# Cross-attention of a perceiver block: row maxima through DRAM, combines of four units, no fills, and masks divided anew among the engines

## The chip, the cores and the metric

The kernel runs on one core of one Trainium2 chip. The metric is device time in microseconds (us). Four runs of the kernel before gave 1000.0, 1001.75, 1003.12 and 1005.47 us; their median is 1002.43. One more execution was profiled.

The engines go by the profile's names: PE is TensorE's matrix multiplication and PEld its loads of the stationary operand, DVE is VectorE, ACT is ScalarE, POOL is GpSimd, SP is SyncE, which here only issues DMAs. "SPq" and "POOLq" are DMA issues of SP and POOL. L916 is line 916 of the kernel before.

## The reference

The program runs a perceiver's two layers in float32: in the first layer a cross-MLP, an attention and a mixture of experts, in the second a cross-attention, an attention by Fourier transforms and a layer of expert heads. The change is in the second layer's cross-attention and at its edges:

```python
# x (2, 256, 256), ctx (2, 4096, 256), mask (1, 1, 256, 4096)
def _L1_xattn_ref(values, keys, queries, mask, w_out, b_out):
    EMBED, HEADS, HEAD_DIM = 256, 16, 16
    v = values.reshape(N, -1, HEADS, HEAD_DIM)      # values = keys = ctx
    k = keys.reshape(N, -1, HEADS, HEAD_DIM)
    q = queries.reshape(N, -1, HEADS, HEAD_DIM)     # queries = layernorm(x)
    energy = jnp.einsum('nqhd,nkhd->nhqk', q, k)
    energy = jnp.where(mask == 0, jnp.float32(-1e+20), energy)
    attn = jax.nn.softmax(energy / math.sqrt(EMBED), axis=3)
    out = jnp.einsum('nhql,nlhd->nqhd', attn, v).reshape(N, q_len, HEADS * HEAD_DIM)
    return out @ w_out.T + b_out
```

So there are 2 x 16 independent softmaxes of 256 queries over 4096 keys, with a head dimension of only 16.

## The kernel before

**Units and steps.** One batch and one head make a unit (`UNITS`, 32 of them). A unit has 4096 keys, held transposed in a tile `keys` of 128 rows: four groups of 32 rows, each with 1024 keys; the group's rows 0 to 15 hold the 16 dimensions of the head and its rows 16 to 31 hold ones. There are five such tiles, filled with ones by POOL at L849, and `load_keys` writes the 16 rows of each group by four DMAs of SP (L857). The queries of a unit lie in a slot of `q0` in the same way, four copies in rows 0 to 15 of the four groups and zeros below (the fill is L869, the DMAs are L884); there are four slots, used in turn. Both loads are made two units ahead, at step 0 of a unit's maxima.

A unit is worked through twice, in eight steps each time.

1. *Maxima* (`max_mms`, L916). In each step two matmuls, on two groups of 32 rows, give 128 queries times 1024 keys in the tile `pm`; one VectorE instruction (L922) adds the mask `maskN` and takes the row maximum. After eight steps L929 reduces these to minus the maximum of each query, two columns for the two blocks of 128 queries. This makes them a row of the queries: ScalarE copies them into `npad` (L930), two TensorE transposes turn that (L937), and VectorE adds the outcome to the unit's queries and writes `q1` (L941). Since the row of `q1` below the 16 dimensions now holds minus the maximum, and the keys hold ones there, the matmul of the energies subtracts the maximum by itself.
2. *Energies* (L1002). In each step four matmuls of two groups give two tiles `pe` of 128 keys x (2 x 256) transposed energies (`step_tiles` says which). There are three PSUM buffers named `pe`; the combines and transposes below take one of them too. ScalarE takes the exponential (L1009) into `e`. The mask then comes in one of three ways: added in PSUM ahead of the energies, by a TensorE matmul of `maskA` with the identity (L979); multiplied in afterwards by VectorE (L987); or multiplied by POOL (L1016). Of the 16 tiles of a unit, 2 went to TensorE (the second tile of steps 1 and 5), 3 to VectorE (the first of steps 0, 3 and 6) and 11 to POOL. Three steps later, eight matmuls (L1033) add the tile's product with the values to `pav`; the values carry a column of ones, which gives the softmax's denominator. The four column groups of `pav` hold four partial sums.

**Finish and combine.** When a unit is through, ScalarE copies `pav` (L946), two matmuls with `stack` sum the four groups and turn the result (L954), VectorE takes the reciprocal of the denominator and multiplies (L958, L959) into `ao`.

**Order.** A loop over T goes through all steps of all units. In each round it issues the mask matmuls of step T, the maxima of step T + 12 (`LEAD`), the energies of step T, a combine that has come due, and the values of step T - 3. A scheduler then orders the instructions of each engine from this program; every engine runs its own list in order. At both ends one of the two kinds of steps runs without the other: maxima alone first, energies alone last. The mask matmuls of the trace stand just ahead of their step's maxima.

**The start of the stage.** The mixture of experts before it ends on TensorE with `py` (L618) and on VectorE with the sum of the gathered expert outputs (L795). `layernorm_T` then normalizes (`xn`, L121), TensorE transposes to `xnT` (L134), and from there the queries go by DMA to `q0`. The output bias `bo` is added to `x` at L1070; the scheduler places its four additions in the ramp, after the normalization, where VectorE waits. After the stage `ao` is transposed and multiplied by `wo`.

Of the kernel before, what the change touches and what calls it, by code (L numbers as in the profile page):

```python
# [9 lines left out]
F32 = mybir.dt.float32  # L10
BF16 = mybir.dt.bfloat16
I32 = mybir.dt.int32
# [7 lines left out]
NT = 4  # L20
# [6 lines left out]
def tile_perceiver(ctx: ExitStack, tc: tile.TileContext, t):  # L27
# [73 lines left out]
    def layernorm_T(es, tag, scale_rows=None, mv=None, then=None, between=None, turn=None):  # L101
# [8 lines left out]
        rstd = sm.tile([P, NT], F32, name="rstd")  # L110
        nc.scalar.activation(rstd, mv[:, :, 1], AF.Sqrt, bias=eps)
        if then is not None:
# [12 lines left out]
        if between is not None:  # L125
            between()
        transpose_tokens(pt, xnT, xn, name)

    def transpose_tokens(pt, dst, src, name="ps_t"):
# [31 lines left out]
    maskN = big.tile([P, 2, S2], BF16, name="maskN")  # L161
    maskA = big.tile([P, 4, S], BF16, name="maskA")
    maskM = big.tile([P, 28, S], I32, name="maskM")
    anyq = big.tile([P, 2], F32, name="anyq")
# [7 lines left out]

    added_tiles = sorted(step_tiles(s)[0][1] * 8 + 2 * step_tiles(s)[1] for s in (1, 5))
    by_vector = [step_tiles(s)[0][0] * 8 + 2 * step_tiles(s)[1] for s in (0, 3, 6)]
    ADDED = {kt: 2 * n for n, kt in enumerate(added_tiles)}
# [5 lines left out]
    xnd = dr.tile([NT * P, D], F32, name="xnd")  # L181
    eod = dr.tile([TILES * P, D], F32, name="eod")

    mla = ExitStack()
# [655 lines left out]
    sig = wh.tile([P, 16], F32, name="sig")  # L840
    with ExitStack() as es:
        sm = pool(es, "xa", 2)
        wk = pool(es, "xa1", 1)
# [3 lines left out]
        for i in range(KEYS):  # L847
            kt_ = wk.tile([P, 1024], F32, name=f"keys{i}")
            nc.gpsimd.memset(kt_, 1.0)  # L849
            kbuf.append(kt_)  # L850

        def load_keys(u):
# [3 lines left out]
            for g in range(4):  # L856
# [3 lines left out]
                )  # L860

        for u in range(2):
            load_keys(u)
        wo = wk.tile([P, 2, D], F32, name="wo")
        nc.sync.dma_start(wo, t["w_outT"].rearrange("(k p) c -> p k c", p=P))
        bo = wk.tile([P, D], F32, name="bo")
        nc.gpsimd.dma_start(bo, t["L1_xattn_b_out"].partition_broadcast(P))
        q0 = wk.tile([P, 4, S], F32, name="q0")
        nc.gpsimd.memset(q0, 0.0)  # L869
        npad = []  # L870
        for i in range(2):
            n_ = wk.tile([P, 2, 4, 32], F32, name=f"npad{i}")
            nc.gpsimd.memset(n_, 0.0)
            npad.append(n_)
        with ExitStack() as es1:
            layernorm_T(es1, "d", scale_rows=anyq, mv=mvd, then=AF.Exp)

        def load_queries(u, queues):
            if u >= len(UNITS):
                return  # L880
            b, h = UNITS[u]
            p0 = (h % 8) * 16
            for g in range(4):
                queues[g % len(queues)].dma_start(  # L884
                    q0[32 * g : 32 * g + 16, u % 4, :], xnT[p0 : p0 + 16, h // 8, b * S : (b + 1) * S]
                )

        for u in range(2):
            load_queries(u, (nc.sync, nc.scalar))
        for j, n in enumerate("qkv"):  # L890
# [8 lines left out]
        pa = p_a.tile([P, S], F32, name="pav")  # L899
        ao = wk.tile([P, NT, D], F32, name="ao")  # L900
        LEAD = 12
        mxs, q1s = {}, {}

        def max_mms(i):

            u, s = divmod(i, 8)
            b, h = UNITS[u]
            qb, c, gp = s // 4, (s // 2) % 2, s % 2
            if s == 0:
                load_keys(u + 2)  # L910
                load_queries(u + 2, (nc.sync,))
                mxs[u] = sm.tile([P, 2, 4], F32, name="mx", bufs=3)
            pm = p_s.tile([P, 2, 512], F32, name="pm")
            for j in range(2):
                g = 2 * gp + j
                nc.tensor.matmul(  # L916
                    pm[:, j, :], lhsT=q0[32 * g : 32 * g + 32, u % 4, qb * P : (qb + 1) * P],
                    rhs=kbuf[u % KEYS][32 * g : 32 * g + 32, c * 512 : (c + 1) * 512], start=True, stop=True,
                )
            junk = sm.tile([P, 2, 512], F32, name="junk", bufs=1)  # L920
            view = maskN[:, qb, :].rearrange("p (g c k) -> p g c k", g=4, c=2)[:, 2 * gp : 2 * gp + 2, c, :]
            nc.vector.tensor_tensor_reduce(  # L922
                out=junk, in0=pm, in1=view, scale=1.0, scalar=-3.0e38, op0=ALU.add, op1=ALU.max,
                accum_out=mxs[u][:, qb, s % 4 : s % 4 + 1],
            )

        def reduce_max_of(u):
            mneg = sm.tile([P, 2], F32, name="mneg")
            nc.vector.tensor_reduce(mneg, mxs.pop(u), axis=AX.X, op=ALU.max, negate=True)  # L929
            nc.scalar.copy(npad[u % 2][:, :, :, 16:17], mneg.unsqueeze(2).unsqueeze(3).to_broadcast([P, 2, 4, 1]))  # L930

        def queries(u):

            b, h = UNITS[u]
            pt = p_e.tile([P, 512], F32, name="pe")[:, 0:S]
            for qb in range(2):
                nc.tensor.transpose(  # L937
                    pt[:, qb * P : (qb + 1) * P], npad[u % 2][:, qb].rearrange("p g w -> p (g w)"), ident
                )
            q1s[u] = sm.tile([P, S], F32, name="q1")  # L940
            nc.vector.tensor_add(q1s[u], pt, q0[:, u % 4, :])  # L941

        def finish(u):
            b, h = UNITS[u]
            av = sm.tile([P, S], F32, name="av", bufs=1)
            nc.scalar.copy(av, pa)  # L946
            return av

        def combine(u, av):
            b, h = UNITS[u]  # L950
            pt = p_e.tile([P, 512], F32, name="pe")
# [12 lines left out]
        later = []  # L964
        done = divided = None
        n_steps = 8 * len(UNITS)
        for T in range(-LEAD, n_steps + 4):
# [30 lines left out]
            if tiles:  # L998
                for j in range(2):
                    for g, kt, pe, added in tiles:  # L1000
                        k0 = (2 * tp + j) * P
                        nc.tensor.matmul(  # L1002
                            pe[:, j * S : (j + 1) * S], lhsT=kbuf[u % KEYS][32 * g : 32 * g + 32, k0 : k0 + P],
                            rhs=q1s[u][32 * g : 32 * g + 32, :], start=not added, stop=(j == 1 or not added),
                        )
# [12 lines left out]
                if T == n_steps - 1:  # L1018
# [4 lines left out]
                    get_ready(AF.Sqrt)  # L1023
            if done is not None:
                divided = combine(*done)
                done = None
            if len(held) == 3 or (held and not tiles):
# [9 lines left out]
                if hs == 7:  # L1037
                    done = (hu, finish(hu))
            if tiles:
                held.append((u, s, now))  # L1040

            if i % 8 == 7 and i < n_steps:
                reduce_max_of(i // 8)
            if i % 8 == 2 and i >= 8 and i // 8 - 1 < len(UNITS):
                queries(i // 8 - 1)

# [13 lines left out]
        if done is not None:  # L1060
            combine(*done)

        transpose_tokens(p_s, xnT, ao, "pm")
        for tt in range(NT):
            po = p_e.tile([P, D], F32, name="pe")
            for k in range(2):
                nc.tensor.matmul(
                    po, lhsT=xnT[:, k, tt * P : (tt + 1) * P], rhs=wo[:, k, :], start=(k == 0), stop=(k == 1)
                )
            nc.vector.tensor_add(x[:, tt, :], x[:, tt, :], bo)  # L1070
            nc.vector.tensor_add(x[:, tt, :], po, x[:, tt, :])
# [416 lines left out]
```

## Time and profile before

| | us |
|---|---|
| median of four runs | 1002.43 |
| the profiled execution | 1000.66 |
| its span, first to last instruction | 998.9 |
| TensorE's mean granted clock in it | 0.956 |

The first part of the profile's page gives each engine's share of the span, the second cuts the span into 40 slices of 25 us (digits are tenths):

```profile
PE 935.0 (94%) x7192; PEld 582.4 (58%) x7192; DVE 641.7 (64%) x1227; ACT 405.5 (41%) x829; POOL 572.1 (57%) x538
...
PE   6999987889993999999999999999999999878997
...
DVE  3333467622216788888888888888888884475342
...
POOL 6322110011014099999999999999999995121830
PEclk9999999799996599999999999999999999997997
```

The cross-attention fills slices 13 to 34. Within its window (322 to 852 us) the groups that the change touches are these; "mean" is one instruction's time:

| line, engine | what | count | busy us | mean ns |
|---|---|---|---|---|
| L1016 POOL | mask product | 344 | 459.6 | 1370 |
| L1002 PE | energies | 2048 | 326.4 | 403 |
| L922 DVE | mask and maximum | 256 | 313.1 | 1223 |
| L916 PE | maxima's products | 1024 | 297.4 | 669 |
| L1009 ACT | exponential | 512 | 278.0 | 595 |
| L1033 PE | weighted values | 2042 | 163.1 | 391 |
| L987 DVE | mask product | 104 | 106.5 | 1025 |
| L979 PE | mask matmul | 64 | 25.1 | 393 |
| L954 PE | combine | 124 | 19.6 | 281 |
| L937 PE | transposes of the maxima | 64 | 14.2 | 305 |
| L941 DVE | maxima added to queries | 32 | 13.3 | 417 |
| L946 ACT | copy of `pav` | 31 | 11.8 | 380 |
| L930 ACT | copy to `npad` | 32 | 6.5 | 205 |

Matmuls of different row groups run beside each other (L916 beside L1002), so busy times of TensorE's lines may add up to more than the window. A timeline's columns are start, length from the first to the last instruction of the row, engine, line, operation, tiles and count.

### The profile page before, as it was taken

What the parts mean: (1) busy time and instruction counts of PE and PEld (TensorE: products, weight loads), DVE (VectorE), ACT (ScalarE), POOL (GpSimd) and SP (SyncE); (2) the same over time, 40 slices, a digit from 0 to 9 for tenths busy, and PEclk for the clock granted to TensorE, in tenths of its full rate; (3) what the DMA queues carried; (4) which work ended last, traced back from release to release, by engine and by line L of the source; (5) the groups of instructions that cost most, each with busy time, mean ns of one, the idle gap of its engine ahead of it and who ended that gap; (6) DMA issues with size and microseconds to landing.
All of it is one profiled execution on the core that took longest, in us unless ns stands there. A gap on an engine that the chain in (4) does not pass through costs nothing.

```text
span 998.9 us, 19042 instructions
## 1 busy us (share of the span) xinstructions
PE 935.0 (94%) x7192; PEld 582.4 (58%) x7192; DVE 641.7 (64%) x1227; ACT 405.5 (41%) x829; POOL 572.1 (57%) x538
## 2 busy tenths in 40 slices
PE   6999987889993999999999999999999999878997
PEld 5888844656661355555555555555555555665455
DVE  3333467622216788888888888888888884475342
ACT  2111247212221055555555556555565555322011
POOL 6322110011014099999999999999999995121830
PEclk9999999799996599999999999999999999997997
DMA  9866400378833201000010000101000000800000
GB/s 304 259 213 211 147 1 2 118 244 286 294 132 86 60 14 28 21 22 22 21 28 19 24 21 21 29 15 28 21 22 22 7 2 2 180 1 0 1 6 16
DMA packets 61121, 73.65 MB, mean 74 GB/s; under 512 B 20273, under 2 KB 48209, under 8 KB 61025
## 3 DMA queue, kind: packets, MB, share of 16 engines
q1 hardware_dynamic: 50384, 57.84, 18.9%
q10 hardware_dynamic: 8864, 10.42, 3.4%
q0 software_dynamic: 1776, 4.12, 1.4%
q8 instruction: 59, 0.97, 0.4%
q14 instruction: 38, 0.30, 0.1%
HBM read 67.24 MB, written 3.01 MB: 70 GB/s over the span
## 4 chain that ended last, share of the span: by engine, by line
PE 71%; DVE 3%; DMA 1%; issue 1%; POOL 1%; ACT 1%; ACTq 0%; SPq 0%; POOLq 0%; DVEq 0%
PE pe L1002 17%; PE pm L916 16%; PE pav L1033 14%; PE pp L1325 4%; PE py L618 3%; PE pe L979 2%; PE ga L593 2%; PE pe L954 2%; PE ua L593 2%; PE pa L1415 1%; PE pe L937 1%; PE gb L593 1%; PE pp L1386 1%; PE pT L607 1%; PE pf L1132 1%
## 5 line engine op out<-in xcount | busy, mean ns | idle before, releaser
L1016 POOL TENSOR_TENSOR e<-e,maskM 128x512 int32<-128x512 int32 x344 | 459.6, 1370 | 77.5 <-ACT e L1009 74.7
L922 DVE CUSTOM_DVE_ANT_1 junk<-pm,maskN 128x1024 f32<-128x1024 f32 x256 | 313.1, 1223 | 81.9 <-PE pe L1002 62.7
L1009 ACT ACTIVATE e<-pe 128x512 f32<-128x512 f32 x512 | 278.0, 595 | 210.5 <-PE pe L1002 210.4
L1002 PE MATMUL pe<-q,keys 32*128 32x256 f32 x2048 | 326.4, 403 | 0.0
L916 PE MATMUL pm<-keys,q 32*128 32x512 f32 x1024 | 297.4, 669 | 6.8 <-DMA q<-xnT 5.5
L1002 PEld LDWEIGHTS pe<-q,keys 32*128 32x128 f32 x2048 | 213.2, 185 | 14.8 <-issue 2.7
L1033 PE MATMUL pav<-e,V 128*32 128x256 f32 x2048 | 163.8, 391 | 0.5 <-POOL e L1016 0.5
L916 PEld LDWEIGHTS pm<-keys,q 32*128 32x128 f32 x1024 | 80.6, 190 | 100.0 <-issue 73.1
L987 DVE SCALAR_TENSOR_TENSOR e<-e,maskM 128x512 f32<-128x512 f32 x104 | 106.5, 1025 | 11.4 <-ACT e L1009 11.4
L1033 PEld LDWEIGHTS pav<-e,V 128*32 128x32 f32 x2048 | 40.7, 108 | 76.6 <-issue 72.0
L377 PE MATMUL ph<-xnT,ct 128*128 128x256 f32 x256 | 63.3, 393 | 1.5 <-ACT xnT L46 1.5
L206 POOL COPY V<-cn 128x256 f32<-128x256 f32 x64 | 26.4, 461 | 64.3 <-DMA cn<-in_ctx 64.3
L351 PE MATMUL acc<-cn,g 128*128 128x256 f32 x256 | 60.3, 379 | 0.0
L382 ACT ACTIVATE g<-ph 128x512 f32<-128x512 f32 x32 | 19.1, 597 | 92.3 <-PE ph L377 70.9
L377 PEld LDWEIGHTS ph<-xnT,ct 128*128 128x128 f32 x256 | 50.6, 198 | 9.2 <-ACT xnT L46 1.9
L351 PEld LDWEIGHTS acc<-cn,g 128*128 128x128 f32 x256 | 48.6, 190 | 6.6
L624 POOL DMA_INDIRECT xg<-xnd,slot_token x9 | 8.6, 960 | 66.3 <-PE px L633 45.1
L1325 PE MATMUL pp<-proj,xnT 128*128 128x512 f32 x96 | 46.4, 642 | 0.0
L1339 POOL TENSOR_TENSOR pw<-pw 128x512 f32<-128x512 f32 (+2 forms) x33 | 27.5, 833 | 23.1 <-DVE pw L1330 21.3
L618 PE MATMUL py<-wd,hT 128*128 128x256 f32 x156 | 38.6, 389 | 1.3 <-issue 1.3
L311 DVE TENSOR_SCALAR maskN<-mi 128x512 bf16<-128x512 int32 x16 | 8.7, 545 | 42.5 <-DMA mi<-in_mask 42.5
L618 PEld LDWEIGHTS py<-wd,hT 128*128 128x128 f32 x156 | 27.8, 189 | 10.5 <-issue 7.8
(383 smaller groups left out, 917.8 us busy)
## 6 DMA issues: line engine op xcount, KB each, us to landing
ct<-in_ctxT SPq DMA_DIRECT2D x8, 1024.0 KB, 6.1
cn<-in_ctx SPq DMA_DIRECT2D x8, 1024.0 KB, 7.9
keys<-in_ctxT SPq DMA_DIRECT2D x128, 64.0 KB, 2.3
wg<-in_L_ffn_we_gate SPq DMA_DIRECT2D x9, 688.0 KB, 6.5
wu<-in_L_ffn_we_up SPq DMA_DIRECT2D x9, 688.0 KB, 6.6
wd<-in_L_ffn_we_down SPq DMA_DIRECT2D x9, 640.0 KB, 4.7
mi<-in_mask ACTq DMA_DIRECT2D x16, 256.0 KB, 4.0
mi<-in_maskT ACTq DMA_DIRECT2D x16, 256.0 KB, 3.4
```

The costliest lines, as they stand in the source:

```text
L351: nc.tensor.matmul(acc[e][qb], lhsT=g[:, j, qb * P : (qb + 1) * P], rhs=cn[:, fc % 8 + j, :], start=(fc + j == 0), stop=(fc + j == NKC - 1),)
L377: nc.tensor.matmul(ph[:, j, :], lhsT=ct[:, k, f0 : f0 + P], rhs=xnT[:, k, e * D : (e + 1) * D], start=(k == 0), stop=(k == 1),)
L593: nc.tensor.matmul(out[:, 0:n], lhsT=xT[k], rhs=m[:, k, f0 : f0 + n], start=(k == 0), stop=(k == 1))
L618: nc.tensor.matmul(py, lhsT=hT[0:m, c, :], rhs=w[2][0:m, c, :], start=(c == 0), stop=(c == NC6 - 1))
L916: nc.tensor.matmul(pm[:, j, :], lhsT=q0[32 * g : 32 * g + 32, u % 4, qb * P : (qb + 1) * P], rhs=kbuf[u % KEYS][32 * g : 32 * g + 32, c * ...
L922: nc.vector.tensor_tensor_reduce(out=junk, in0=pm, in1=view, scale=1.0, scalar=-3.0e38, op0=ALU.add, op1=ALU.max, accum_out=mxs[u][:, qb, ...
L987: mul = nc.vector.scalar_tensor_tensor(e, e, 3.0e38, maskM[:, KEPT[kt] : KEPT[kt] + 2, :], op0=ALU.min, op1=ALU.mult)
L1002: nc.tensor.matmul(pe[:, j * S : (j + 1) * S], lhsT=kbuf[u % KEYS][32 * g : 32 * g + 32, k0 : k0 + P], rhs=q1s[u][32 * g : 32 * g + 32, :] ...
L1009: nc.scalar.activation(e.rearrange("p j q -> p (j q)"), pe, AF.Exp, scale=1.0 / 16.0)
L1016: nc.gpsimd.tensor_tensor(ei, ei, maskM[:, KEPT[kt] : KEPT[kt] + 2, :], ALU.mult)
L1033: nc.tensor.matmul(pa[32 * n : 32 * n + 32, :], lhsT=V[:, hb * NKC + kt + j, 17 * hh : 17 * hh + 32], rhs=e[:, j, :], start=(hs == 0), sto ...
L1325: nc.tensor.matmul(pp[:, hf * 512 : (hf + 1) * 512], lhsT=xnT[:, k, tt * P : (tt + 1) * P], rhs=proj[:, j, k, hf * 512 : (hf + 1) * 512], ...
```

## The change

Six things change in the stage.

1. *Maxima.* Minus the maximum is written into column 0 of a 32-wide block, VectorE transposes 32x32 blocks, SP writes the four rows to a DRAM tile `maxd` and, from there, reads a row of 256 into row 16 of each group of `q0`. The energies read `q0` itself; `npad`, `q1`, the two TensorE transposes, the ScalarE copy and the addition go. `q0` has five slots (`QN`); from unit 5 on one more DMA sets row 16 of the new slot back to zeros. The loads of unit u + 2 are issued at step 3 of unit u's maxima, no longer at step 0.
2. *Combine.* `pav` is copied into a slot of `av4`. After every fourth unit, four matmuls with `stack` as the stationary operand sum four units at once, into the four column groups; ScalarE copies the sum, two transposes turn it, and VectorE divides all four units in one pair of instructions. The last four units are combined one at a time as before. `ao` lies in `xn`'s place.
3. *Fills.* POOL's fills go. The keys' rows of ones come by 20 DMAs from a DRAM tile `onesd`, two of them issued by SP and 18 by POOL; ScalarE writes the zeros of `q0`. The keys' tiles come from a pool of their own, opened first.
4. *First queries.* Unit 0's queries come to `q0` by a padded copy, eight matmuls with the identity and one copy out of PSUM. Unit 1's come by DMA as before.
5. *Masks.* Of the 16 tiles of a unit, 4 go to TensorE (the first tile of steps 1, 3, 5 and 7), 1 to VectorE (the first of step 6) and 11 to POOL.
6. *Bias.* The four additions of `bo` are issued after the first unit's reduction of the maxima.

```diff
-    added_tiles = sorted(step_tiles(s)[0][1] * 8 + 2 * step_tiles(s)[1] for s in (1, 5))
-    by_vector = [step_tiles(s)[0][0] * 8 + 2 * step_tiles(s)[1] for s in (0, 3, 6)]
+    added_tiles = sorted(step_tiles(s)[0][0] * 8 + 2 * step_tiles(s)[1] for s in (1, 3, 5, 7))
+    by_vector = [step_tiles(6)[0][0] * 8 + 2 * step_tiles(6)[1]]
...
-            kt_ = wk.tile([P, 1024], F32, name=f"keys{i}")
-            nc.gpsimd.memset(kt_, 1.0)
-            kbuf.append(kt_)
+            kbuf.append(kp.tile([P, 1024], F32, name=f"keys{i}"))
...
+        def set_ones(i, queues):
+            for g in range(4):
+                queues[g % len(queues)].dma_start(
+                    kbuf[i][32 * g + 16 : 32 * g + 32, :],
+                    onesd.rearrange("a b -> (a b)").unsqueeze(0).to_broadcast([16, 1024]),
+                )
...
             load_keys(u)
+            set_ones(u, (nc.sync, nc.gpsimd) if u == 0 else (nc.gpsimd,))
...
-        nc.gpsimd.memset(q0, 0.0)
-        npad = []
...
+            if u >= QN:
+                queues[0].dma_start(
+                    q0[16:P:32, u % QN, :], zerosd.rearrange("a b -> (a b)").unsqueeze(0).to_broadcast([4, S])
+                )
...
+        with tc.issue_after(rooted.ins):
+            nc.scalar.mul(q0[:, 1:, :], ones[:, 0:1].unsqueeze(2).to_broadcast([P, QN - 1, S]), 0.0)
+        load_queries(1, (nc.sync, nc.scalar))
+        for i in range(2, KEYS):
+            set_ones(i, (nc.gpsimd,))
...
+        nc.vector.tensor_copy(pad[:, :, 0:16], xn[:, 0:2, 0:16])
+        pt = p_e.tile([P, 512], F32, name="pe")[:, 0:S]
+        for qb in range(2):
+            for g in range(4):
+                nc.tensor.matmul(
+                    pt[32 * g : 32 * g + 32, qb * P : (qb + 1) * P], lhsT=pad[:, qb, :], rhs=ident,
+                    start=True, stop=True,
+                )
+        nc.vector.tensor_copy(q0[:, 0, :], pt)
...
-            if s == 0:
+            if s == 3:
                 load_keys(u + 2)
                 load_queries(u + 2, (nc.sync,))
+            if s == 0:
...
-            nc.scalar.copy(npad[u % 2][:, :, :, 16:17], mneg.unsqueeze(2).unsqueeze(3).to_broadcast([P, 2, 4, 1]))
...
+            last_max = nc.vector.tensor_reduce(mneg[:, :, 0], mxs.pop(u), axis=AX.X, op=ALU.max, negate=True)
+            rows = sm.tile([P, 2, 32], F32, name="mrows")
+            nc.vector.transpose(rows.rearrange("p t i -> p (t i)"), mneg.rearrange("p t i -> p (t i)"))
+            nc.sync.dma_start(maxd[u].rearrange("(t n i) -> n t i", t=2, n=4), rows[0:P:32])
+            nc.sync.dma_start(q0[16:P:32, u % QN, :], maxd[u].unsqueeze(0).to_broadcast([4, S]))
...
+        def finish(u):
+            nc.scalar.copy(av4[:, u % 4, :], pa)
+
+        def combine_four(u):
+            pt = p_e.tile([P, 512], F32, name="pe")[:, 0:S]
+            for n in range(4):
+                nc.tensor.matmul(pt[32 * n : 32 * n + 32, :], lhsT=stack, rhs=av4[:, n, :], start=True, stop=True)
+            avs = sm.tile([P, S], F32, name="avs")
+            nc.scalar.copy(avs, pt)
+            return avs
+
+        def divide_four(u, avs):
...
             for qb in range(2):
+                nc.tensor.transpose(pt[:, qb * P : (qb + 1) * P], avs[:, qb * P : (qb + 1) * P], ident)
+            ptv = pt.rearrange("p (t n w) -> p t n w", t=2, n=4)
+            den = sm.tile([P, 2, 4], F32, name="den4")
+            nc.vector.reciprocal(den, ptv[:, :, :, 16])
...
-                            rhs=q1s[u][32 * g : 32 * g + 32, :], start=not added, stop=(j == 1 or not added),
+                            rhs=q0[32 * g : 32 * g + 32, u % QN, :], start=not added, stop=(j == 1 or not added),
...
+            if summed is not None:
+                divided = divide_four(*summed)
+                summed = None
+            if done is not None and done >= len(UNITS) - 4:
+                divided = combine(done)
+            elif done is not None and done % 4 == 3:
+                summed = (done, combine_four(done))
...
-            if i % 8 == 2 and i >= 8 and i // 8 - 1 < len(UNITS):
-                queries(i // 8 - 1)
+                if i == 7:
+                    with tc.issue_after(last_max.ins):
+                        for tt in range(NT):
+                            nc.vector.tensor_add(x[:, tt, :], x[:, tt, :], bo)
```

`tc.issue_after(ins)` makes the scheduler place what follows behind that instruction. In the built program VectorE takes the reduction, one of the four additions, the 32x32 transpose, then the other three; and TensorE's list has 15.5 steps of maxima ahead of the first energies, where it had 12.

## The prediction

> **What bounds the kernel now.** I began with the chain of waits, which tells the engine that sets the end.
>
> ```profile
> PE 71%; DVE 3%; DMA 1%; issue 1%; POOL 1%; ACT 1%; ACTq 0%; SPq 0%; POOLq 0%; DVEq 0%
> ```
>
> The same part of the page gives the lines on the chain: L1002 (energies) 17%, L916 (maxima) 16%, L1033 (weighted values) 14%. That is the cross-attention, from the first maximum at 322.46 to about 852 us. Next I cut windows inside it (columns: busy us and count of PE, weight loads, DVE, ACT, POOL, then the granted clock).
>
> ```profile
> 310.00:350.00 40.00, 28.58 (x91) 11.90 (x93) 26.12 (x40) 2.96 (x7) 6.72 (x10) 0.50 0.27 69
> 352.00:354.00 2.00, 2.00 (x28) 1.23 (x22) 1.33 (x4) 1.37 (x3) 2.00 (x3) 1.00 0.03 8
> 600.00:700.00 100.00, 100.00 (x1067) 56.40 (x1063) 85.10 (x146) 57.84 (x115) 93.19 (x70) 1.00 0.09 23
> ```
>
> In the steady part TensorE never pauses, GpSimd is close behind, VectorE is not. So TensorE's list of work, and its hidden stalls, must be counted by the step. I read that from its timeline.
>
> ```profile
> 700.95 0.70 PE L916 MATMUL pm<-keys,q 32*128 32x512 f32 x2
> ...
> 702.75 0.39 PE L979 MATMUL pe<-maskA,identb 128*128 128x512 bf16 x1
> 703.08 0.70 PE L916 MATMUL pm<-keys,q 32*128 32x512 f32 x2
> ...
> 704.72 0.70 PE L916 MATMUL pm<-keys,q 32*128 32x512 f32 x2
> ...
> 706.12 0.64 PE L1033 MATMUL pav<-e,V 128*32 128x256 f32 x8
> 706.69 0.44 PE L937 MATMUL pe<-ident,npad 128*128 128x128 f32 x2
> 707.05 0.70 PE L916 MATMUL pm<-keys,q 32*128 32x512 f32 x2
> ...
> 715.62 0.63 PE L954 MATMUL pe<-stack,av 128*128 128x32 f32 x4
> 716.18 0.64 PE L1033 MATMUL pav<-e,V 128*32 128x256 f32 x8
> 716.75 0.70 PE L916 MATMUL pm<-keys,q 32*128 32x512 f32 x2
> ```
>
> A unit is 716.75 - 700.95 = 15.80 us (over six units, 606.11 to 700.95, 15.81). A mask on TensorE takes 703.08 - 702.75 = 0.33, the transposes of the maxima 0.36, the combine 0.56. Step 5, from 703.08 to 704.72, has nothing extra: 1.64. Eight such steps (13.12), two masks (0.66), 0.36 and 0.56 make 14.70; the other 1.10 are stalls, with TensorE counted busy: step 6 lasts to 706.69, or 1.97, so 0.33 of stall. The second energies tile of a step needs a PSUM buffer (there are three) whose exponential (595 ns, L1009) has to end. In the eight steps shown the step right after a masked one loses 0.30 to 0.33, and a masked step or one after a stall little or nothing.
>
> **The change part by part.** Sums are made against the profiled execution, 1000.66 us (span 998.9), 1.8 us under the median of 1002.43, to which I add the result.
>
> *Masks, transposes, combine.* Per unit the transposes go (-0.36), two masks come (+0.66). Masks now stand in steps 1, 3, 5 and 7, so every even step follows a masked one. A pair costs 1.64 + 0.33 (masked, no stall) and 1.64 + 0.31 (stalled): 3.92, four pairs 15.70 (with one more digit kept). A unit's combine of 0.56 becomes one of four matmuls of 256 columns for four units, on four column groups. The trace has no such group: from below, one L1033 step of the same 256 columns, 8 matmuls in 0.57; from above the four in sequence by L1033's mean of 391 ns, 1.56. I take 0.57, since L1033 also uses 32 columns at a time. Two transposes follow it (0.21 net, inside L134's 1.86 for seven, 0.27 each). Together 0.78 (at most 1.93) a four, 0.19 (0.48) a unit: 15.89 against 15.81, +0.08. Over the 27 units in the even stretch, with the 3-unit tail left out, +2.3 us (at most +10; if even steps lost only the 0.16 that step 4, behind the combine, loses now, 4 x 0.15 less a unit, -14). Units 28 to 31 still combine singly; 0.56 that takes the place of 0.15 of a stall makes 15.70 + 0.41 = 16.11, +0.30 in each of the three with maxima beside them, +0.9. The tail without maxima has two more masks per unit, less the transposes and a stall: +0.3. Steady part: **+3.5**.
>
> *GpSimd and VectorE.* GpSimd keeps 11 of 16 mask products a unit: 11 x 1.37 (L1016) = 15.07, under 15.9, so it stays second. VectorE loses two L987 (2 x 1.03) and the addition of the maxima (0.42 at L941), and gains a 32x32 transpose (no row; between the 0.16 of the L929 reduction and the 0.42 of L941). It was busy 85% and held nothing up, so this is worth nothing by itself; the cover is TensorE's 100%.
>
> *Maxima through DRAM.* Now the reduction of a unit (L929 at 606.34) starts 2.4 us after the step 3 beside it (606.11 less that step's 2.20); its 0.16 and the transpose's 0.2 to 0.4 bring this to 2.8 to 3.0. Then SyncE issues a write to DRAM and, when that has landed, a read back to four partitions. Nearest rows from issue to landing: keys 2.3, queries 1.8; above them the MoE's writes to DRAM, median 3.2 late in that stage, 4.6 over all. With two trips of 2.0 the rows are there at about 7.0; the first energies that read them start five steps after that step's start, 3 x 1.64 + 2 x 2.28 (start to start, mask and stall included) = 9.5. So 2.5 us to spare. SyncE issues 11 DMAs a unit where it had 8; behind the waiting pair stand only loads for a unit two ahead (due about 25 us later), and TensorE waits for none of them. Cost nothing at 2.0 a trip; the cover ends at 3.2 a trip, and each further us costs 2 x 31 = 62 us in all. No row excludes it, so it is a rival.
>
> The Trainium skill, "DMA: Bandwidth & Descriptors" (the anatomy of one DMA), gives about 2.0 us fixed to a transfer, mostly the receipt of the write, and slower for writes to DRAM under load. That agrees with 1.8 to 2.3 in the rows and speaks against a chain of two with the wait on it; by it the chain would still end at 7.0.
>
> *The start.* Before, the fills hold VectorE's normalization and the first key loads.
>
> ```profile
> 308.32 4.52 POOL L849 MEMSET keys<- 128x1024 f32 x5 [3.93 <-DVE mvd L99]
> 308.94 6.70 DVE L121 TENSOR_SCALAR xn<-x,mvd,rstd 128x256 f32<-128x256 f32 x4
> 317.40 2.77 ACTq L884 DMA_DIRECT2D q<-xnT  x4
> 319.91 2.73 SPq L884 DMA_DIRECT2D q<-xnT  x4
> 322.46 2.33 PE L916 MATMUL pm<-keys,q 32*128 32x512 f32 x8 [5.55 <-DMA q<-xnT]
> ```
>
> Four of these VectorE operations took 1.38 us in the first layer's normalization, here 6.70. Without fills xn is ready near 310.3, its transposes near 311.7; unit 0's queries come by eight small matmuls and a copy instead of four DMAs (issue 317.40, use 322.46). First maximum near 313.4, 9 us sooner. But the built order puts 15.5 steps of maxima before the first energies, where it was 12, because unit 0's rows go through DRAM; steps 0 to 2 of the energies then have no maxima beside them. At half clock two steps of maxima alone take 3.41 us (324.77, 328.18, 331.59). So 15 x 1.71 = 25.6, plus 1.5 for three additions of the bias now among them on VectorE (1.43 for four at L1070) and 2 for the first steps' fill: first energies near 342.4 (344.23 before), first weighted values near 352.4 (352.64 before). Ones and zeros by 20 DMAs, 18 of them on GpSimd's queue, at 0.59 each (the bo load at 312.79), 10.6 us; its first mask product is needed past 342, which covers them. The clock may come back later, since the first energies load TensorE less: it came 7.5 us after 344.23, and three thinner steps would put that to about 355, half of 3.4 lost: +1.7; or not at all: 0. I take **+1**; bounds -9 (whole head start kept) to +4.
>
> The Trainium skill, "TensorE: Matmul & The Clock Gate" (the gate), says that some 3.4 us of busy TensorE restore the full clock. The trace differs: maxima ran from 322.46 and the clock stood at 0.50 until 351.7. By the rule the ramp after the change would run at full speed from about 317 and end some 4 to 10 us sooner. I go by the trace.
>
> Sum: 3.5 + 1 = 4.5: 1005.2 for an execution like the profiled one, **1002.43 + 4.5 = 1006.9 us** by the median.
>
> **The rivals.**
> *(a) The head start is kept* (chance 0.25). For it: PE waits 5.55 for queries and 9.80 for xn, both gone; maxima done early need not be done later. Against it: maxima beside energies cost no time of their own (701.48 and 701.50 run together), so doing them early and alone buys nothing. If the ramp ends 9 us sooner, 1002.43 + 3.5 - 9 = 997; with stalls at 0.16 too, about 983 (then GpSimd, at 15.07 plus its gaps, holds).
> *(b) The pair of DMAs comes late* (0.13). In the steady part, at the first energies of each unit, in front of which TensorE then idles with GpSimd and ACT behind it. Decides from 3.2 us a trip; at 3.4 a trip 2 x 0.2 x 31 = +12, 1019; at 4.6, +87, 1093. For it: 4.6 for writes to DRAM; against it, those were 128 KB and 21 GB/s is all that moves here.
> *(c) The clock comes late* (0.07). Another 8 us at half rate in the ramp cost 4: 1010 to 1012.
> The forecast itself, work on TensorE exchanged for nearly as much, has 0.55, from 1000 to 1010.
>
> **How the numbers follow.** No change means within 0.5%, or 5 us either way (997.4 to 1007.4). Of the forecast's 0.55 some 0.33 fall there and 0.22 above; (a) gives 0.25 faster, of which 0.02 is within; (b) and (c) 0.20 slower. Faster 0.24, same 0.35, slower 0.41. Range 993 to 1020: the head start half kept at the bottom, trips of 3.4 at the top, with about 0.2 outside; the forecast's own range is 1000 to 1010.
>
> **What would show it.** A unit's period of 15.85 to 15.95, stalls of 0.3 in even steps and none in masked ones; combine at 0.6 and transposes at 0.2 once in four units. Energies of step 0 without a wait for q's DMA; if they have one, (b). xn's four operations near 1.4 us, first maximum near 313, first weighted values near 352 with the clock at 0.50 until then; values before 346 would show (a), a clock below 1.00 after 356 (c). A period under 15.6 would make the forecast wrong in its stall count.

## The result and the profile after

The changed kernel takes 1004.05 us (median of 52 runs, 1000.48 to 1009.32) where the kernel before takes 1001.26 (78 runs): a ratio of 1.0025, 95% interval 1.0018 to 1.0032. It is slower by 2.5 us by the ratio (2.8 between the medians), clear of the noise of so many runs, and within the half per cent that the prediction counts as no change. 1006.9 was forecast, +4.5: the direction came, the size was little more than half of it. Of all runs reported below, one of the kernel with the queries by DMA stood apart, at 1168.59 us with a granted clock of 0.73; its ratio leaves it out.

The first part of the page of the changed kernel, the shares of the span, shows that much moved although the time hardly did: VectorE lost 88 us of work (641.7 before), TensorE gained 11 (935.0), GpSimd lost 8 (572.1). (A part of VectorE's loss is waiting that it counted as work; the last section has the lines.)

```profile
PE 945.8 (94%) x7166; PEld 573.2 (57%) x7166; DVE 553.8 (55%) x1121; ACT 401.9 (40%) x805; POOL 563.8 (56%) x552
```

Windows of the changed kernel (busy us and count of PE, PEld, DVE, ACT, POOL, then granted clock, DMA share, GB/s):

```profile
311.00:314.50 3.50, 3.13 (x24) 2.07 (x24) 1.92 (x6) 2.13 (x4) 2.01 (x5) 0.50 1.05 179
314.50:318.00 3.50, 1.97 (x10) 0.97 (x12) 1.91 (x4) 0.00 (x0) 2.32 (x5) 0.99 1.11 196
318.00:340.00 22.00, 21.34 (x52) 6.17 (x48) 17.09 (x32) 0.00 (x0) 0.00 (x0) 0.50 0.38 96
340.00:349.60 9.60, 9.18 (x30) 4.92 (x28) 1.28 (x4) 3.15 (x6) 4.30 (x4) 0.50 0.01 2
349.60:355.50 5.90, 5.90 (x39) 2.79 (x38) 2.32 (x5) 1.90 (x5) 3.21 (x3) 0.50 0.01 3
600.00:700.00 100.00, 100.00 (x1058) 53.65 (x1054) 69.14 (x124) 57.22 (x111) 89.71 (x71) 1.00 0.09 22
```

In the steady part TensorE is as full as before (100.00 of 100), VectorE fell from 85 to 69. The relief is all on an engine that held nothing up. The ramp stands at half clock until 355.5 (351.7 before), with a single stretch at full clock, just behind the dense transposes of 311 to 314.

Some lines of TensorE's timeline in the changed kernel, around a combine of four units:

```profile
707.54 0.70 PE L947 MATMUL pm<-keys,q 32*128 32x512 f32 x2
...
709.18 0.70 PE L947 MATMUL pm<-keys,q 32*128 32x512 f32 x2
...
711.12 0.39 PE L1027 MATMUL pe<-maskA,identb 128*128 128x512 bf16 x1
711.44 0.70 PE L947 MATMUL pm<-keys,q 32*128 32x512 f32 x2
...
717.00 0.70 PE L947 MATMUL pm<-keys,q 32*128 32x512 f32 x2
...
718.88 0.39 PE L1027 MATMUL pe<-maskA,identb 128*128 128x512 bf16 x1
719.20 0.70 PE L947 MATMUL pm<-keys,q 32*128 32x512 f32 x2
...
732.02 0.64 PE L978 MATMUL pe<-av,stack 128*32 128x256 f32 x8
732.48 0.61 PE L1087 MATMUL pav<-e,V 128*32 128x256 f32 x8
...
734.39 0.44 PE L987 MATMUL pe<-ident,avs 128*128 128x128 f32 x2
734.75 0.62 PE L1087 MATMUL pav<-e,V 128*32 128x256 f32 x5
```

The step from 707.54 to 709.18 has its mask behind it and lasts 1.64; the next, to 711.44, holds a stall and the following step's mask: 2.26 = 1.64 + 0.32 + 0.30. Step 4, from 717.00 to 719.20, stalls for 0.24 only. The combine takes 0.46, its two transposes 0.36.

And the start, all engines, in the changed kernel:

```profile
310.54 1.43 DVE L121 TENSOR_SCALAR xn<-x,mvd,rstd 128x256 f32<-128x256 f32 x4
...
313.18 1.08 PE L928 MATMUL pe<-ident,pad 128*32 128x128 f32 x16
314.86 1.47 PE L947 MATMUL pm<-keys,q 32*128 32x512 f32 x8 [0.59 <-issue]
...
331.54 0.57 SPq L964 DMA_DIRECT2D q<-maxd  x1
...
340.12 1.22 PE L1050 MATMUL pe<-q,keys 32*128 32x256 f32 x2
```

Where the time of the two profiled executions went can be read from these points. All but the last, the end of the span, are starts or ends of TensorE instructions; "unit 2" and "unit 29" are the first weighted values of the second and of the twenty-ninth unit, and the period is the mean of the 27 units between them.

| us | before | after | difference of the stretch |
|---|---|---|---|
| end of the experts' `py` | 303.34 | 304.19 | +0.85 |
| first maximum | 322.46 | 314.86 | |
| first energies | 344.23 | 340.12 | |
| first weighted values | 352.64 | 351.66 | |
| unit 2 | 368.42 | 368.79 | -0.48 since `py` |
| unit 29 (period) | 795.23 (15.81) | 795.71 (15.81) | +0.11 |
| end of weighted values | 852.65 | 854.74 | +1.61 |
| end | 998.92 | 1002.23 | +1.22 |

Inside the stage that is -0.48 + 0.11 + 1.61 = +1.24; the last four units alone cover it. The +0.85 ahead of it and the +1.22 behind it lie where the edit changes next to nothing: over the kernels below, whose code behind the stage is nearly the same, the last stretch alone took 145.7 to 151.5 us. In it the granted clock stands at 0.50 for 35.7 us in the trace after and for 30.7 in the trace before; 5 us more at half the rate can cost up to 2.5, an estimate that is enough for the 1.22. What part of the measured 2.5 us is due to that can't be told from one profile each.

### The profile page after: what moved, and what is told of

Its sections match the earlier page's. It is cut to its first block, busy times and chain, and to the rows that moved or that the text cites. A ratio compares the mean times of both kernels' runs of the same rounds, so it can differ in the third digit from the quotient of the medians.

```text
span 1002.2 us, 19028 instructions
## 1 busy us (share of the span) xinstructions
PE 945.8 (94%) x7166; PEld 573.2 (57%) x7166; DVE 553.8 (55%) x1121; ACT 401.9 (40%) x805; POOL 563.8 (56%) x552
## 5 line engine op out<-in xcount | busy, mean ns | idle before, releaser
L1064 POOL TENSOR_TENSOR e<-e,maskM 128x512 int32<-128x512 int32 x348 | 448.8, 1310 | 87.8 <-ACT e L1057 66.3
L1050 PE MATMUL pe<-q,keys 32*128 32x256 f32 x2048 | 331.7, 405 | 0.4 <-ACT e L1057 0.4
L390 ACT ACTIVATE g<-ph 128x512 f32<-128x512 f32 x32 | 19.1, 597 | 90.8 <-PE ph L385 85.3
L1027 PE MATMUL pe<-maskA,identb 128*128 128x512 bf16 x128 | 50.3, 393 | 0.0
L1027 PEld LDWEIGHTS <-identb 128*128 128x128 bf16 x128 | 12.2, 95 | 53.5 <-issue 53.5
```

Source lines behind the costliest of these rows:

```text
L1027: nc.tensor.matmul(pe, lhsT=identb, rhs=maskA[:, ADDED[kt] : ADDED[kt] + 2, :].rearrange("p j q -> p (j q)"), start=True, stop=False,)
L1050: nc.tensor.matmul(pe[:, j * S : (j + 1) * S], lhsT=kbuf[u % KEYS][32 * g : 32 * g + 32, k0 : k0 + P], rhs=q0[32 * g : 32 * g + 32, u % QN ...
L1064: nc.gpsimd.tensor_tensor(ei, ei, maskM[:, KEPT[kt] : KEPT[kt] + 2, :], ALU.mult)
```

## The experiments

Theory A: TensorE's list of work sets the steady period; what the transposes and the combines free there, the two added mask matmuls take back. And the head start of the new beginning is lost because the built order puts 15.5 steps of maxima ahead of the first energies. Rivals: the other engines or the stalls set the period (B), the trip through DRAM costs hidden time, the clock eats the start.

All times are medians, ratios are against the kernel before on the same chip.

**Masks back.** The changed kernel with the old division of masks.

```diff
-    added_tiles = sorted(step_tiles(s)[0][0] * 8 + 2 * step_tiles(s)[1] for s in (1, 3, 5, 7))
-    by_vector = [step_tiles(6)[0][0] * 8 + 2 * step_tiles(6)[1]]
+    added_tiles = sorted(step_tiles(s)[0][1] * 8 + 2 * step_tiles(s)[1] for s in (1, 5))
+    by_vector = [step_tiles(s)[0][0] * 8 + 2 * step_tiles(s)[1] for s in (0, 3, 6)]
```

> The changed kernel with the masks divided as before it (2 of 16 on TensorE, 3 on VectorE, 11 on GpSimd), all else as changed. Theory A (TensorE's list sets the period; the two added mask matmuls give back what the transposes and combines freed): 8 x 1.645 + 0.65 + 0.21 + about 1.2 of stalls = 15.2 us a unit instead of 15.81, about 18 us in all, 983 to 990 us. Theory B (with the freed time gone, GpSimd's 11 products of 1.31 to 1.37 us, 14.4 to 15.1, or VectorE set the period soon): 15.5 to 15.8 a unit and no more than 8 us gained, 993 to 1002.

989.52 us, ratio 0.988 (0.9852 to 0.9907); period 15.31. Theory A in the main. The window and two groups of this run show how near the next bounds are:

```profile
500.00:700.00 200.00, 197.87 (x2151) 108.61 (x2147) 185.55 (x282) 118.03 (x226) 193.69 (x145) 1.00 0.10 24
```

```profile
L1064 POOL TENSOR_TENSOR e<-e,maskM 128x512 int32<-128x512 int32 x344 | 461.8, 1371 | 57.3 <-ACT e L1057 52.2
...
L1035 DVE SCALAR_TENSOR_TENSOR e<-e,maskM 128x512 f32<-128x512 f32 x104 | 136.9, 1317 | 13.7 <-ACT e L1057 13.7
```

TensorE is now idle for 1%, GpSimd busy 97%, VectorE 93%; the three are nearly level. In this window TensorE's idle time is 2.1 us, 0.16 a unit, and all of it waits for VectorE's maxima:

```profile
PE pm L947 <- DVE mx L953: 2.1, 10, 0.3
```

That covers the 0.11 by which the period came out above the 15.2 worked out from TensorE alone. VectorE's product takes 1317 ns on average, where it took 1025 before (L987).

**Masks alone.** The kernel before with the new division, the reverse of the diff above.

> The kernel before with the new division of the masks alone (4, 1, 11). Theory A: two mask matmuls of 0.33 more on a full TensorE, less up to 0.2 of stalls: 16.25 to 16.5 us a unit, 14 to 21 us slower, 1015 to 1023. Theory B (the products on VectorE held TensorE up, so freeing VectorE pays for the matmuls): 15.8 or less, 1002 or less.

1020.11 us, ratio 1.0186 (1.0162 to 1.021); period 16.35, 0.54 over the kernel before. Theory A again: the new division of masks by itself costs 18.6 us (medians), 0.54 a unit; with the rest of the change it costs 0.50 (15.81 against 15.31).

**Single combines.** The changed kernel with a combine for each unit.

```diff
-            if done is not None and done >= len(UNITS) - 4:
+            if done is not None:
                 divided = combine(done)
```

> The changed kernel with every unit combined by itself as before the change, all else as changed. Theory A: the period is that of the last units, 16.09, against a mean of 15.81: 28 x 0.28 = 8 us slower than the changed kernel, 1010 to 1014. Theory B (the combine falls into stalls that are there anyway): no slower than the changed kernel by more than 2 us.

1013.52 us, ratio 1.0119 (1.0091 to 1.0146); period 16.08. The combine of four is worth 0.27 a unit.

**Maxima on TensorE.** The changed kernel with the old way of the maxima.

```diff
-            rows = sm.tile([P, 2, 32], F32, name="mrows")
-            nc.vector.transpose(rows.rearrange("p t i -> p (t i)"), mneg.rearrange("p t i -> p (t i)"))
-            nc.sync.dma_start(maxd[u].rearrange("(t n i) -> n t i", t=2, n=4), rows[0:P:32])
-            nc.sync.dma_start(q0[16:P:32, u % QN, :], maxd[u].unsqueeze(0).to_broadcast([4, S]))
+            nc.scalar.copy(npad[u % 2][:, :, :, 16:17], mneg.unsqueeze(2).unsqueeze(3).to_broadcast([P, 2, 4, 1]))
...
+            if i % 8 == 2 and i >= 8 and i // 8 - 1 < len(UNITS):
+                queries(i // 8 - 1)
```

> The changed kernel with the maxima turned by two TensorE transposes, a ScalarE copy and a VectorE addition as before it, no DRAM; the earlier loads and five slots stay. Theory A: 0.36 a unit comes back, of which a stall swallows 0.1 to 0.2: 15.97 to 16.17 a unit, 5 to 11 us slower than the changed kernel in the steady part; in the start the first energies no longer wait for DRAM in the built order, which may give back up to 5: 1005 to 1015. Theory B (the way through DRAM costs hidden waits): faster than the changed kernel, under 1003.

1002.88 us, ratio 1.0014 (0.9983 to 1.0044). Neither theory alone: the period is 16.07, 0.26 more than with DRAM, 7 us over the stage; but the first energies come at 336.73 (340.12 with DRAM), the first weighted values at 344.74 (351.66) and unit 2 at 360.59 (368.79), 8 us sooner. The way through DRAM gains 7 in the steady part and loses 8 in the start.

**Energies held in order.** The changed kernel; the first matmul of each step of maxima from T = 1 to 8 is held behind everything issued to TensorE before it, so that 12.5 steps of maxima precede the first energies.

```diff
+                if 0 < T <= 8 and j == 0:
+                    tc.keep_in_program_order(mm)
```

> The changed kernel with TensorE's first eight steps of energies held in program order, so that they come after 12.5 steps of maxima instead of 15.5; nothing else. Theory A (the built order, not the trip through DRAM, eats the head start; the row of unit 0 was written by about 334 us and first read at 340): first energies near 336, second unit's first weighted values near 361.5 instead of 368.8, 6 to 8 us faster than the changed kernel, 995 to 999. Theory B (the trip is late there): TensorE waits ahead of the first energies until about 340 and no more than 2 us are gained.

993.93 us, ratio 0.993 (0.9908 to 0.9952). First energies at 335.74, unit 2 at 359.53, period 15.81. Theory A: the row of unit 0 was there; only the order had the energies wait. In windows of this run the granted clock returns 6 us after the energies have joined the maxima:

```profile
310.00:335.00 25.00, 21.96 (x72) 8.11 (x72) 17.05 (x34) 2.61 (x4) 4.70 (x10) 0.50 0.62 126
335.00:342.00 7.00, 7.00 (x37) 4.60 (x36) 4.37 (x8) 2.17 (x4) 2.85 (x3) 0.51 0.19 54
342.00:350.00 8.00, 8.00 (x86) 4.43 (x83) 5.81 (x11) 4.68 (x9) 7.90 (x7) 1.00 0.01 3
```

**Both.** Masks back and energies held in order.

> The changed kernel with both: masks 2, 3, 11 as before and the first energies held in program order. If the two effects stand on different stretches they add: 989.5 - 7 = 981 to 985. If the fuller VectorE and GpSimd take the earlier start back, 988 to 991.

978.11 us, ratio 0.9767 (0.9736 to 0.9799). The effects add: the two ratios, 0.988 and 0.993, against 1.0025 of the changed kernel make 0.9785, within the interval. The 3 us under the expected range are no more than that interval. The run beats both kernels by over 2%.

**The start alone.** Masks, combines and maxima as before the change; of the change the fills, the first queries, the later loads, the five slots and the place of the bias additions are left.

> Only the new start: no fills, unit 0's queries through TensorE, later loads, five slots; masks 2, 3, 11, combines by unit and maxima by TensorE transposes as before. Theory A: first maximum 7.5 us sooner and all of it kept, since the first energies come 12.5 steps later as before: 992 to 996. Theory B (time ahead of the energies buys nothing, since the clock or the filling of the pipeline sets the first weighted values): 999 to 1003.

994.4 us, ratio 0.994 (0.9921 to 0.9958). Unit 2 comes 56.1 us after the end of `py`, before 65.1. Theory A: the head start can be kept whole.

**A dense matmul beside the maxima.**

```diff
+            if i < LEAD:
+                tc.keep_in_program_order(nc.tensor.matmul(
+                    p_e.tile([P, 512], F32, name="pe"), lhsT=identb,
+                    rhs=maskA[:, 0:2, :].rearrange("p j q -> p (j q)"), start=True, stop=True,
+                ))
```

> As the run with masks back and first energies in program order, and one more matmul of 128 rows and 512 columns (bf16, its product is read by nobody) after each of the first 12 steps of maxima. Theory C (matmuls of 32 rows do not lift the granted clock, one on all 128 rows in each step does): clock 1.00 through the ramp, steps of 1.4 instead of 1.7 us, the first energies at full rate: 5 to 7 us faster than that run, 975 to 979. Theory D (the clock is held down by something else): at half clock each costs 0.5 to 0.6, 6 to 7 us slower than that run.

984.46 us, ratio 0.9833 (0.9817 to 0.985): 6.4 slower than without, as theory D had it. One row of a window and two of the timeline of this run:

```profile
310.00:345.00 35.00, 32.90 (x83) 9.38 (x83) 18.09 (x38) 3.32 (x5) 5.95 (x12) 0.50 0.50 100
```

```profile
319.87 0.61 PE L954 MATMUL pe<-maskA,identb 128*128 128x512 bf16 x1
320.41 2.08 PE L947 MATMUL pm<-keys,q 32*128 32x512 f32 x4
```

From the first maximum (315.21) to the first energies TensorE is busy without a gap, and the clock stays at 0.50; it returns at 349.7, 3.8 us after the first energies (345.89). A fifth of the time in matmuls over all rows does not lift it.

**The last four at once.** The run with both edits, and units 28 to 31 combined together, divided after the loop.

> Masks back, first energies in program order, and the last four units combined at once like the others, no longer one by one. Three units lose about 0.4 us each of single combines (15.85 and 15.38 against 15.2), and the end of the stage gets one copy and two transposes longer, about 1: 0 to 1 us faster than the same without it (978.1), 976 to 979. If the longer end counts more, 979 to 981.

977.99 us, ratio 0.9779 (0.9755 to 0.9802). The same within the interval; the single combines at the end are not worth a second form of code.

**One and two trips more.** The changed kernel with the energies held in order through all steps, and the maxima copied once or twice in DRAM on their way.

```diff
             nc.sync.dma_start(maxd[u].rearrange("(t n i) -> n t i", t=2, n=4), rows[0:P:32])
+            nc.sync.dma_start(hop[0][u], maxd[u])
+            nc.sync.dma_start(hop[1][u], hop[0][u])
-            nc.sync.dma_start(q0[16:P:32, u % QN, :], maxd[u].unsqueeze(0).to_broadcast([4, S]))
+            nc.sync.dma_start(q0[16:P:32, u % QN, :], hop[1][u].unsqueeze(0).to_broadcast([4, S]))
```

> The changed kernel with its energies held in program order (993.9) and the maxima copied once more in DRAM, write, copy, read, so that each unit's row comes one trip of 1.7 to 2.0 us later. From the trace of the changed kernel the row is there at about 706.2 and used at 709.2. Theory A (3 us to spare hide the trips): 0 to 2 slower than without the copy, 993 to 996, period 15.81. Theory B (the trip is already on the path): 1.7 x 31 = 50 slower.

994.91 us, ratio 0.9936 (0.9919 to 0.9954), period 15.81: hidden.

> The same with two copies in DRAM. Two trips of 1.7 to 2.0 make 3.4 to 4.0, over the 3.0 to spare: TensorE waits 0.4 to 1.0 us at the first energies of each unit, 12 to 31 us, and up to 2 in the start: 1006 to 1027. If the spare time is larger than read, no slower than 997.

1019.67 us, ratio 1.0175 (1.015 to 1.02), period 16.67, so 0.86 a unit. Lines of TensorE, of SyncE's queue and of two windows from this run:

```profile
704.82 1.13 PE L1055 MATMUL pe<-q,keys 32*128 32x256 f32 x8 [0.42 <-DMA q<-hop]
```

```profile
713.59 0.59 SPq L966 DMA_DIRECT2D maxd<-mrows  x1
715.24 0.53 SPq L967 DMA_DIRECT2D hop<-maxd  x1
717.17 0.50 SPq L968 DMA_DIRECT2D hop<-hop  x1
719.13 0.55 SPq L969 DMA_DIRECT2D q<-hop  x1
```

```profile
630.00:637.00 7.00, 5.93 (x57) 2.90 (x59) 5.53 (x9) 3.26 (x6) 5.38 (x4) 1.00 0.09 22
637.00:644.00 7.00, 7.00 (x47) 3.29 (x45) 1.23 (x2) 2.17 (x4) 3.39 (x3) 0.51 0.10 29
```

Each issue waits for the landing of the one before it, so a trip is 1.65, 1.93 and 1.96 us here (medians over the 32 units: 1.64, 1.83 and 1.90), and the spare time lies between one and two copies more. Of the 0.86 a unit, 0.21 stands in the trace as waits of TensorE for `q<-hop` (5.7 us, nine waits in the 27 units). The longest, 1.07 us just before 636.62, was followed by 6.8 us at half clock, worth up to 3.4. The rest, over half, lies where TensorE is counted busy and was not taken apart.

**Unit 0's queries by DMA.** The changed kernel with energies held in order; the padded copy, the eight matmuls and the copy go, four DMAs bring the queries, and ScalarE writes the zeros of unit 0's slot too.

```diff
-        load_queries(1, (nc.sync, nc.scalar))
+        for u in range(2):
+            load_queries(u, (nc.sync, nc.scalar))
```

> The changed kernel with its energies held in program order and unit 0's queries by four DMAs as before the change, no longer through TensorE. Theory A (each part of the start counts for itself): from issue to use these DMAs took 5 us, the matmuls and the copy 1.7: 3 to 4 us slower than with the matmuls, 997 to 998. Theory B (the fills alone held the start): within 1 of 993.9.

1003.21 us, ratio 1.0014 (1.0002 to 1.0026): 9 us slower than with the matmuls, where 3 to 4 were expected. The kind was right and the size wrong; the timeline of this run shows why:

```profile
308.82 0.31 SPq L864 DMA_DIRECT2D keys<-in_ctxT  x1
...
312.35 2.52 ACTq L896 DMA_DIRECT2D q<-xnT  x4
...
317.45 0.31 SPq L864 DMA_DIRECT2D keys<-in_ctxT  x1
318.18 0.39 SPq L880 DMA_DIRECT2D wo<-in_w_outT  x1
318.67 2.51 SPq L896 DMA_DIRECT2D q<-xnT  x4
...
321.63 2.42 PE L938 MATMUL pm<-keys,q 32*128 32x512 f32 x8 [9.45 <-DMA q<-xnT]
```

What SyncE's load of the keys waited for (us in total, times, longest):

```profile
SPq L864 <- DMA q<-xnT: 8.3, 1, 8.3
```

Half of the queries go by ScalarE's queue at 312.35. SyncE's half is issued at 318.67, 6.3 us later, because two loads stand ahead of it in SyncE's order: the last load of unit 1's keys waits for the semaphore of ScalarE's first query DMA, and that of `wo` for the semaphore of its second. The first of these DMAs, among the rows of ones with the DMA engines 96% busy (308 to 318), is done only 5.1 us after its issue (317.45 less 312.35). Without the fills, but with the queries by DMA, the first maximum comes 18.9 us after the end of `py`, hardly sooner than before (19.1). So the head start comes from the queries through TensorE, with the fills' removal as its condition as far as xn is concerned; fills with the queries through TensorE were not tried.

## Why the prediction was right and wrong

**The bound** was read rightly: TensorE at 100% in the steady part, so that only its own list counts. VectorE's loss of 16 points of load was worth nothing, as priced.

**The steady period** is the step that failed: the mechanism held, and this term of the sum was mis-sized. 15.89 against 15.81 was worked out, +2.3 us over 27 units; the measured period is 15.81 and the stretch +0.11. Four pairs of steps were put at 15.70; a unit without a combine measures 15.595, or 3.90 a pair. The even steps stall for 0.29 on average and not for 0.31 (step 4 for 0.24), and a mask costs 0.32 and not 0.33. The combine with its transposes costs 0.85 a four (0.78 predicted: 0.46 and 0.36 measured, with 0.03 in stalls). The difference of two sums near 15.8 was smaller than what the reading of the stalls could carry: an error of 0.7% in the pairs is the whole 2.3 us.

The parts, one by one, stand for less than their durations:

| part | TensorE time counted, us a unit | measured by undoing it, us a unit |
|---|---|---|
| two more mask matmuls | +0.66 | +0.50 (alone in the old kernel: +0.54) |
| transposes of the maxima gone | -0.36 | -0.26 |
| combine of four for four combines | -0.37 | -0.27 |

All three shrink by about a quarter. That a part of each stood in, or now fills, a stall is an inference; in the run with masks back, 0.16 a unit is waiting for VectorE. So they also cancel: +0.50 - 0.26 - 0.27 = -0.03. What maxima and combines freed on TensorE, 0.53 a unit, the new division of masks spent.

**The last four units** were put at +0.9 and +0.3, and came to +1.31 and +0.30. Of the +1.31, 0.40 is the second half of the combine of units 24 to 27, which falls past the end of the even stretch; the single combines themselves came as priced.

**The start** was put at +1, and measured -0.48 from the end of `py` to unit 2, or +0.37 by the clock of the trace. First maximum 314.86 (313.4 predicted), first energies 340.12 (342.4), first weighted values 351.66 (352.4), clock back at 355.5 (355). So +1 was mis-sized too, by 1.5. The mechanism held: counted from the end of `py`, the changed kernel leads by 8.4 us at the first maximum, by 5.0 at the first energies, by 1.8 at the first weighted values and by 0.5 at unit 2. The steps of maxima ahead of the energies eat the first part of the lead, the energies that run without maxima at half clock the rest. Before the change, TensorE had 13 steps ahead by the trace (52 matmul records, four a step) and not 12, so 2.5 were added. What the prediction did not ask is whether that order was needed. It took the order as a consequence of the trip through DRAM; the row was issued for its last trip at 331.5, and holding the order gave 9 us back.

**The rivals.** (a) was right in its mechanism and not in this kernel: maxima done early need not be done later, provided that the energies follow sooner too. The prediction's objection, that early maxima buy nothing by themselves, explains the changed kernel; two runs (993.9 and 994.4) show the head start kept. (b) was weighed rightly: a trip costs 1.65 to 2.0, one more is hidden, two more are not. The spare time of 2.5 that was worked out lies between those two. (c) did not come: the clock was back at 355.5. Two slips in the numbers changed nothing: the parts of the chances make faster 0.23 and slower 0.42, and 993 as the range's foot lies below the 997 that (a) has for the whole head start, so it can't stand for half of it.

**On the clock.** The Trainium skill, "TensorE: Matmul & The Clock Gate" (the gate), has full clock after some 3.4 us of a busy TensorE. None of these ramps agrees: 22 us of maxima at 0.50 in the changed kernel with TensorE 97% busy, 30 us at 100% with a dense matmul in each step. The prediction went by the trace of before, and rightly.

Open: the stage itself has 1.24 us of the measured 2.5, in one profile of each kernel; how much of the rest is the change's, and how much the clock's ahead of the stage and behind it, was not settled.

## What to carry to other kernels

Where one engine is full, add up its own list for each part of a change before combining parts: here 0.53 us a unit was freed and 0.50 spent in one edit, and leaving the spending out made the kernel 12 us faster than before the change, with the order of the start held 23. A longer path to the first result costs little by itself; look at how the scheduler moves work in front of the wait, and hold the order if the data are there in time. And a duration taken out of a list with stalls in it was worth about three quarters of itself here.

## What the runs showed of the hardware

- The granted clock stayed at 0.50 with TensorE 97% busy in maxima on 32 rows each (318 to 340 in the changed kernel), 96% busy in energies with two mask matmuls (340 to 349.6), and 100% busy with a 128-row matmul in a fifth of the time. It returned 3.8 us (345.89 to 349.7) to 10.4 us (343.99 to 354.4, masks alone) after energies and maxima began to run together. In every trace here the stretches at one clock are multiples of 3.41 us long, but for the last, which the trace's end cuts (11 of them from 318.0 to 355.5 in the changed kernel), so a return can only fall on such a grid. What exactly the gate counts was not settled.
- In the run with two copies more, a wait of 1.07 us in the steady part was followed by 6.8 us at half clock (from 637.2).
- A DMA of 1 KB from SBUF to DRAM took 1.65 us from its issue to the issue that waits for it, one from DRAM to DRAM 1.93 (medians over the units 1.64 and 1.83).
- VectorE's mask product (two inputs in SBUF) took 1025 ns on average before the change and 1317 with masks back, but 689 in the changed kernel, with GpSimd 90% busy there too. So GpSimd's load doesn't set it: what counts is whether a GpSimd product is running when it starts. In the kernel before (VectorE and GpSimd):

```profile
701.25 1.30 POOL L1016 TENSOR_TENSOR e<-e,maskM 128x512 int32<-128x512 int32 x1
701.56 1.54 DVE L987 SCALAR_TENSOR_TENSOR e<-e,maskM 128x512 f32<-128x512 f32 x1
...
707.04 0.69 DVE L987 SCALAR_TENSOR_TENSOR e<-e,maskM 128x512 f32<-128x512 f32 x1
707.19 1.68 POOL L1016 TENSOR_TENSOR e<-e,maskM 128x512 int32<-128x512 int32 x1 [0.45 <-ACT e L1009]
...
710.27 1.30 POOL L1016 TENSOR_TENSOR e<-e,maskM 128x512 int32<-128x512 int32 x1
711.12 1.01 DVE L987 SCALAR_TENSOR_TENSOR e<-e,maskM 128x512 f32<-128x512 f32 x1
```

  The first and the last of VectorE's end 0.55 us after the GpSimd product beside which they started (703.10 after 702.55, 712.13 after 711.57); the second, which starts with none running, takes 0.69, and the GpSimd product that starts beside it takes 1.68 instead of 1.30. Of the 104 of the kernel before, 64 start beside a running one, all of which end 0.55 to 0.67 us after it, and the other 40 take 0.68 to 0.69. So one engine waits for the other and the profile counts the wait as busy.
- One queue can wait for another's transfers through a shared semaphore: in the run with the queries by DMA SyncE stood from 309.1 to 317.5 behind a DMA that ScalarE had issued at 312.35.
